# Attention weights times v in eighths of the TensorE array: blocks of 32 keys by 64 queries, four PSUM banks, keys in even and odd blocks, v by way of memory, and a new placing of all steps

## The chip, the cores and the metric

The kernel runs on one core of one Trainium2 chip. The metric is the device time of one execution in microseconds (us), and the time shown for a kernel is the median of its runs. The program is written by hand for the five engines of a core: PE (TensorE, matrix multiplies), DVE (VectorE), ACT (ScalarE), POOL (GpSimd) and SP (SyncE, which here issues all the transfers).

## The reference

The input is 2048 tokens of 128 channels. Twelve transformer layers (six, then a linear-attention block, then the same six again) work on it. One of the twelve layers, cut to what matters here:

```
def local_attention(q, k, v):            # 16 heads of 64; windows of 32 tokens
    bk2, bv2 = look(bk), look(bv)        # each window sees itself and the window before
    sim  = einsum('bhwie,bhwje->bhwij', bq, bk2) * 8.0     # 32 queries x 64 keys
    sim  = where(mask, -max, sim)        # key at most the query, and at most 32 back
    attn = softmax(sim, -1)
    out  = einsum('bhwij,bhwje->bhwie', attn, bv2)         # weights times v

def attn_layer(x, Wqkv, qs, ksc, Wo):
    q, k, v = split(x @ Wqkv)            # each 2048 x 1024
    q, k = l2norm(q) * qs, l2norm(k) * ksc, both rotated
    return local_attention(q, k, v) @ Wo

for i in range(6):
    x = attn_layer(shift_tokens(x), ...) + x
    x = ffn_layer(shift_tokens(x), ...) + x      # layer norm, gated GELU
```

The change is in the last line of `local_attention` and in what prepares its operands. Everything is float32, but for a band mask in bf16.

## The kernel before

Activations lie transposed, channels on the 128 partitions. A layer is worked in 8 chunks of 256 tokens (`AC`), a chunk in 4 steps: two halves of 128 tokens, `t`, times two groups of 8 heads, `h8`. Twelve layers of 32 steps make 384 steps. A feed-forward block of 512 tokens is spread over 8 steps (two chunks), so the work repeats every 8 steps.

For each step the kernel does, in the functions named: `project` (L288) multiplies one quarter of q and k out of the activations into two PSUM tiles, p0 for q and p1 for k; DVE multiplies each by the rotary table (`prod`, L297), POOL adds the halves (`abq`, `abk`, L303), ACT squares them (L309) and POOL adds the squares (L323), whose sums over channels `square_sums` takes on PE (`ss`, L331). `values_proj` (L347) computes half of v for 128 tokens, and ACT copies it (L351). `similarities` puts the mask (L475) and then q times k (L485) into two PSUM tiles, and DVE takes the maxima (L497, L498). `exponentials` (L510) is called for each of the two tiles: four ACT instructions each, called e0 and e1 below. `normalised` divides (`e`, L522, POOL), `transposed` turns the weights on PE (`te`, L535) and copies them (`eT`, L541). `values` (L562) multiplies weights by v into PSUM tiles `av`, which ACT and DVE copy to `oT` (L569, L571). In every second step `output` (L578) multiplies `oT` by Wo into `y`. The feed-forward's matmuls are `mean`, `var`, three gates and three ups `pf` (L612), and `yf` (L637).

In `values` the array is used as four tiles of 64 rows by 64 columns. One instruction takes 64 keys and 32 queries of one head; 32 of them make a step. The trace shows two passes for each, since float32 takes two. v has to lie on the partitions of the keys of each query window; `values_windows` makes these shifted copies by eight transfers from SBUF to SBUF for each 128 tokens.

Every PSUM tile but the similarities and the square sums comes from one pool of five banks:

```
ps_small = ctx.enter_context(tc.tile_pool(name="ps_small", bufs=5, space=PSUM))
def small(name):
    return ps_small.tile([P, CH], F32, tag="small", name=name)
```

A matmul that opens a tile waits until the last reader of the bank's earlier tile is done. The similarities have two banks, that is one pair, so the next step's mask waits for e0 and e1 of this one.

The order on each engine is written out by hand: the table `POS` gives each piece of each function a step, counted from its chunk's, and a place in that step; pieces are emitted in the order of these numbers, and every engine runs its instructions in that order. A generator's pieces go in turn whatever their own numbers say. In the kernel before, a step's places run: `ss` 25, `pv` 26, rotary products and squares of the projection before 42 to 48, `te` 62, `sim` 73, v's copy 90, e0 95, e1 96, `e` 108, `y` 112, `av` 149, the next projection 150, POOL's square sums 156, the copies of `av` 189 and 190.

Of the kernel before, what the change touches and what calls it, by code (L numbers as in the profile page):

```python
# [15 lines left out]
P = 128  # L16
# [17 lines left out]
    "tabq": [(-11, 129), (-10, 188)],  # L34
    "tabk": [(-9, 19), (-9, 166)],
    "ss": [(-6, 25)],
    "vwin": [(0, 76)],
    "gq0": [(-6, 100)],
    "gq1": [(-4, 78)],
    "e0": [(0, 95)],  # L40
    "e1": [(0, 96)],
    "nrm": [(1, 108)],
    "qn": [(-3, 127)],
    "ek": [(-1, 91)],
    "proj": [(-9, 150), (-8, 42), (-8, 44), (-8, 45), (-8, 48), (-8, 156)],
    "vproj": [(-2, 26), (-2, 90)],
    "norms": [(-4, 47), (-4, 82), (-4, 125)],
    "rk": [(-4, 206), (-3, 27)],
    "sk0": [(-2, 94)],
    "sk1": [(-1, 176)],  # L50
    "te": [(2, 62), (2, 64)],
    "av": [(2, 149), (2, 189), (2, 190)],
    "out": [(4, 112), (4, 134)],
    "sim": [(0, 73), (0, 74), (0, 75)],
    "ff": [(11, 101), (12, 34), (12, 106), (13, 7), (13, 170), (14, 131), (15, 124), (15, 143),
        (16, 17), (16, 42), (16, 143), (16, 159), (17, 51), (17, 140), (17, 192), (18, 50),
        (18, 58), (18, 148), (18, 162), (21, 146), (21, 199)],
    "ff2": [(12, 128), (12, 194), (13, 179), (14, 65), (14, 99), (15, 52), (15, 118), (15, 147),
        (16, 20), (16, 23), (16, 122), (16, 123), (16, 130), (16, 151), (16, 152), (16, 153),
        (16, 203), (17, 5), (17, 40), (17, 97), (17, 169)],  # L60
    "ff3": [(10, 182), (10, 184), (10, 186), (10, 194), (10, 198), (10, 200), (10, 204), (11, 2),
        (11, 4), (11, 13), (11, 24), (11, 35), (11, 36), (11, 37), (11, 120), (11, 133),
        (11, 139), (11, 157), (11, 181), (11, 183), (11, 193)],
    "start0": [(-19, 114), (-17, 104), (-16, 84), (-16, 168), (-13, 41), (-10, 79)],
    "start1": [(-11, 126), (-9, 70), (-7, 31), (-7, 142), (-7, 158), (-6, 141)],
    "start2": [(-9, 19), (-7, 29), (-5, 136), (-5, 205), (-4, 11), (-4, 121)],
    "start3": [(-4, 12), (-4, 16), (-4, 46), (-4, 88), (-3, 6), (-2, 28)],
    "sums0": [(-9, 1), (-9, 49), (-8, 43), (-8, 165), (-8, 174), (-7, 43), (-7, 137), (-6, 30)],
    "sums1": [(-1, 92), (-1, 119), (0, 72), (0, 77), (1, 38), (1, 39), (2, 161), (2, 184)],
    "sums2": [(1, 185), (1, 201), (2, 167), (2, 202), (3, 63), (3, 93), (3, 160), (4, 113)],  # L70
    "sums3": [(3, 195), (4, 15), (4, 80), (4, 81), (4, 144), (4, 145), (4, 177), (4, 191)],
    "kv": [(5, 3)],
    "outs0": [(5, 9), (5, 14), (5, 109), (5, 111), (5, 173), (5, 175), (6, 54), (6, 68), (6, 71),
        (6, 138), (7, 55), (7, 61), (7, 69), (7, 135)],
    "outs1": [(6, 60), (11, 83), (11, 110), (12, 18), (13, 53), (13, 67), (13, 180), (14, 98),
        (14, 163), (15, 32), (15, 56), (15, 102), (15, 154), (17, 87)],
    "outs2": [(6, 10), (13, 21), (13, 89), (13, 164), (14, 171), (14, 178), (14, 196), (15, 33),
        (15, 116), (15, 143), (16, 66), (16, 85), (16, 132), (17, 22)],
    "outs3": [(5, 172), (15, 115), (15, 155), (16, 117), (17, 86), (17, 105), (18, 8), (18, 103),
        (18, 107), (18, 162), (18, 197), (19, 57), (19, 59), (19, 187)],  # L80
# [14 lines left out]
def kernel(ctx: ExitStack, tc: tile.TileContext, a: dict, out: bass.AP):  # L95
# [65 lines left out]
    band = keep([P, 2, SK], "band", BF16, a["band"])  # L161
# [111 lines left out]
    def project(l, c, g):  # L273
# [8 lines left out]
        xs = xa[:, c * AC : (c + 1) * AC]  # L282
        both = []
        for s in range(2):
            ps = small(f"p{s}_{nm}")
            both.append(ps.rearrange("p (u t) -> p u t", u=2))
            for u in range(2):
                nc.tensor.matmul(  # L288
                    both[s][:, u, :], wqk[g][:, 2 * s + u, :], xs, start=True, stop=True
                )  # L290
# [46 lines left out]
    def values_proj(l, c, i):  # L337
# [5 lines left out]
        if j == 0:  # L343
            d["v", t] = work.tile([P, INNER], F32, tag="v", name=f"v_{nm}", bufs=3)
# [8 lines left out]
    def values_windows(l, c, t):  # L353


        d = chunk(l, c)
        ti = 2 * c + t
        nm = f"{d['nm']}_{t}"
        v = d["v", t]
        w = work.tile([P, 3, CH], F32, tag="vw", name=f"vw_{nm}", bufs=2)  # L360
        vp = None if ti == 0 else d["v", 0] if t else chunks[l, c - 1]["v", 1]
        for u in range(2):
            r, cols = 64 * u, slice(CH * u, CH * u + CH)
            if ti == 0:
                nc.gpsimd.memset(w[r : r + 32, 0, :], 0.0)
            else:
                nc.sync.dma_start(w[r : r + 32, 0, :], vp[96:P, cols])
            nc.sync.dma_start(w[r + 32 : r + 64, 0, :], v[0:32, cols])
            nc.sync.dma_start(w[r : r + 64, 1, :], v[32:96, cols])
            nc.sync.dma_start(w[r : r + 64, 2, :], v[64 - r : P - r, cols])  # L370
        d["vs", t] = [
            [w[0:64, 0], v[0:64, 0:CH], w[0:64, 1], w[0:64, 2]],
            [w[64:P, 0], w[64:P, 2], w[64:P, 1], v[64:P, CH:]],
        ]

    def gather(l, c, qk, g2):
# [3 lines left out]
        off = 0 if qk == "q" else WIN  # L380
        if g2 == 0:
            d["h" + qk] = work.tile(
                [P, 8, off + AC], F32, tag=f"h{qk}", name=f"h{qk}_{d['nm']}"
            )
        for j in range(2):
            src = d[qk, g2][64 * j : 64 * j + 64]
            first = 4 * g2 + 2 * j
            if qk == "q":
                nc.sync.dma_start(
                    d["hq"][:, first : first + 2, :].rearrange("p i t -> p (i t)"),  # L390
                    src.rearrange("p u i t -> p u (i t)"),
                )
            else:
                for i in range(2):
                    nc.sync.dma_start(d["hk"][:, first + i, WIN:], src[:, :, i, :])
# [54 lines left out]
    def earlier_keys(l, c):  # L450

        d = chunk(l, c)
        first = d["hk"][:, :, 0:WIN]
# [5 lines left out]
        nc.tensor.matmul(ps3, rot_m, chunks[l, c - 1]["hk"][:, :, AC:], start=True, stop=True)  # L459
        nc.scalar.copy(first, ps3)  # L460

    def similarities(l, c, step):
# [8 lines left out]
        masks = [(0, b) for b in range(4)] + [(1, 0)] * (2 * c + t == 0)  # L471
        for m, b in masks:
            for par in range(2):
# [4 lines left out]
                    start=(m == 0), stop=False, skip_group_check=True,  # L478
                )
        for i in range(4):  # L480
            for b in range(4):
                for par in range(2):
                    rows = slice(64 * par, 64 * par + 64)
                    at = t * P + WIN * b
                    nc.tensor.matmul(  # L485
                        sims[par][WIN * b : WIN * b + WIN, i, :],
                        d["hq"][rows, 4 * h8 + i, at : at + WIN],
                        d["hk"][rows, 4 * h8 + i, at : at + SK],
# [11 lines left out]
    def exponentials(l, c, step, par):  # L500
        d = chunk(l, c)
        t, h8 = divmod(step, 2)
        if par == 0:
            d["e", step] = work.tile(
                [P, 4, 2, SK], F32, tag="e", name=f"e_{d['nm']}_{step}", bufs=3
# [3 lines left out]
        for i in range(4):  # L509
            nc.scalar.activation(  # L510
                e[:, i, par, :], d["sims", step][par][:, i, :], AF.Exp,
# [5 lines left out]
    def normalised(l, c, step):  # L517
# [3 lines left out]
        ef = d["e", step].rearrange("p i r k -> p (i r) k")  # L521
# [435 lines left out]
```

## Time and profile before

| | |
|---|---|
| median of 3 runs (lowest, highest) | 3454.14 us (3449.54, 3456.67) |
| the profiled execution: its time, its span | 3449.61 us, 3447.8 us |
| mean granted TensorE clock | 0.982 of full speed |
| busy share of the span: PE, DVE, ACT, POOL | 96%, 77%, 72%, 63% |
| moved by DMA | 459.91 MB, 133 GB/s over the span |

The span is the time from the first to the last instruction; the execution is 1.8 us longer. A row of the groups of instructions gives engine, operation, output and inputs with their shapes, the count, the busy time, the mean time of one, and the idle time of the engine before them with what ended it. In a timeline, rows give start, length, engine, line, operation and count. PEld is the weight load of a matmul, which the trace keeps apart.

### The profile page before, as it was taken

To read this page: it belongs to the slowest core of one execution; us is meant where nothing else is said; L and a number is where in the kernel's file an instruction comes from. 1 tells how busy PE (TensorE), PEld (TensorE's weight loads), DVE (VectorE), ACT (ScalarE), POOL (GpSimd) and SP (SyncE) were. 2 spreads that over 40 slices of the span, in tenths; PEclk is the share of its full clock that TensorE was granted. 3 is DMA by queue.
4 is the path that set the end of the run, shared out by engine and by line. 5 is a ranking of instruction groups with operands and counts; after the bars stand their busy time and mean duration, and the time that the engine had idled before them with its cause. 6 is when DMAs were issued, how large, how long until landed. Compare 5 with 4: busy or idle time off the path is not lost. (4 is left out here: it accounts for less than half of the span.)

```text
span 3447.8 us, 153348 instructions
## 1 busy us (share of the span) xinstructions
PE 3293.9 (96%) x64088; PEld 2280.2 (66%) x64088; DVE 2658.6 (77%) x5068; ACT 2491.0 (72%) x8613; POOL 2182.2 (63%) x2195
## 2 busy tenths in 40 slices
PE   6999999999999999999678999999999999999998
PEld 3776776676667676676334766766767766766665
DVE  5787888878778788786446887887878888787785
ACT  4777777777777777776446777777777777777775
POOL 6766666667667667663136766666666666666661
PEclk8999999999999999999889999999999999999999
DMA  4665565556556556554004665566565565565552
GB/s 134 145 150 135 141 152 142 136 150 147 133 146 153 132 143 156 139 135 121 28 13 100 144 150 142 135 153 147 133 153 143 135 153 142 139 150 138 144 134 73
DMA packets 356445, 459.91 MB, mean 133 GB/s; under 512 B 52396, under 2 KB 218664, under 8 KB 355752
## 3 DMA queue, kind: packets, MB, share of 16 engines
q1 hardware_dynamic: 355752, 450.11, 53.7%
q8 instruction: 504, 8.26, 1.0%
q14 instruction: 189, 1.55, 0.1%
HBM read 96.53 MB, written 2.62 MB: 29 GB/s over the span
## 5 line engine op out<-in xcount | busy, mean ns | idle before, releaser
L510 ACT ACTIVATE e<-sim,st,rq 128x64 f32<-128x64 f32 x3072 | 1196.0, 410 | 352.6 <-DVE st L498 322.8
L297 DVE TENSOR_TENSOR prod<-p,tab 128x1024 f32<-128x1024 f32 x768 | 936.1, 1222 | 293.4 <-ACT sq L309 202.1
L288 PE MATMUL p<-xa,wqk 128*128 128x256 f32 x3072 | 776.5, 395 | 13.6 <-DVE xa L242 4.8
L303 POOL TENSOR_TENSOR abq<-prod 128x512 f32<-128x512 f32 x384 | 490.7, 1278 | 398.3 <-DVE prod L297 364.3
L522 POOL TENSOR_TENSOR e<-e,st 128x512 f32<-128x512 f32 x384 | 451.8, 1177 | 425.5 <-DVE st L520 242.8
L309 ACT ACTIVATE sq<-p 128x512 f32<-128x512 f32 x768 | 438.8, 603 | 350.5 <-PE ss L331 159.2
L303 POOL TENSOR_TENSOR abk<-prod 128x512 f32<-128x512 f32 x384 | 492.4, 1282 | 242.6 <-DVE prod L297 217.8
L510 ACT ACTIVATION_READ_ACCUMULATOR e<-sim,st,rq 128x1 f32 x3072 | 643.3, 209 | 0.0
L288 PEld LDWEIGHTS p<-xa,wqk 128*128 128x128 f32 x3072 | 557.7, 191 | 105.8 <-issue 9.8
L323 POOL TENSOR_TENSOR sq<-sq 128x256 f32<-128x256 f32 x768 | 580.1, 776 | 0.2
L562 PEld LDWEIGHTS av<-eT,vw 64*64 64x64 f32 x18432 | 392.3, 135 | 227.8 <-ACT hk L460 59.6
L562 PE MATMUL av<-eT,vw 64*64 64x32 f32 x18432 | 434.9, 221 | 2.9 <-DVE eT L541 1.8
L347 PE MATMUL pv<-wv,xa 128*128 128x512 f32 x768 | 417.5, 626 | 7.8 <-DVE oT L571 7.8
L578 PE MATMUL y<-oT,wo 128*128 128x128 f32 x3072 | 390.5, 280 | 0.2 <-DVE oT L571 0.2
L578 PEld LDWEIGHTS y<-oT,wo 128*128 128x128 f32 x3072 | 362.5, 192 | 36.1 <-issue 22.6
L562 PE MATMUL av<-eT,v 64*64 64x32 f32 x6144 | 384.3, 219 | 0.0
L535 PEld LDWEIGHTS te<-sq_consts,e 128*128 128x128 f32 x1536 | 188.5, 141 | 236.1 <-issue 166.9
L497 DVE TENSOR_REDUCE sim<-sim 128x4 f32<-128x256 f32 x768 | 325.9, 424 | 21.6 <-PE sim L485 20.7
L485 PE MATMUL sim<-hk,hq 64*32 64x64 f32 x24576 | 333.3, 223 | 0.1
L562 PEld LDWEIGHTS av<-eT,v 64*64 64x64 f32 x6144 | 318.8, 135 | 0.0
L612 PE MATMUL pf<-xc,w 128*128 128x512 f32 (+1 forms) x576 | 304.6, 615 | 11.5 <-POOL xc L600 9.3
L485 PEld LDWEIGHTS sim<-hk,hq 64*32 64x32 f32 x24576 | 306.0, 105 | 0.3
(140 smaller groups left out, 4270.9 us busy)
## 6 DMA issues: line engine op xcount, KB each, us to landing
hq<-abq SPq DMA_DIRECT2D x384, 256.0 KB
hk<-abk SPq DMA_DIRECT2D x768, 128.0 KB
vw<-v SPq DMA_DIRECT2D x768, 128.0 KB
rk<-rkd SPq DMA_DIRECT2D x384, 128.0 KB
vw<-v SPq DMA_DIRECT2D x744, 64.0 KB
wqk<-in_Wqk SPq DMA_DIRECT2D x48, 256.0 KB
tab<-in_rot SPq DMA_DIRECT2D x24, 512.0 KB
wv<-in_Wv SPq DMA_DIRECT2D x24, 256.0 KB
```

The costliest lines, as they stand in the source:

```text
L288: nc.tensor.matmul(both[s][:, u, :], wqk[g][:, 2 * s + u, :], xs, start=True, stop=True)
L297: nc.vector.tensor_tensor(prod, both[s].unsqueeze(2).to_broadcast([P, 2, 2, AC]), tabs[l, s].rearrange("p (u v) t -> p u v t", u=2), ALU.mult,
L303: nc.gpsimd.tensor_tensor(d["qk"[s], g // 2][:, :, g % 2, :], prod[:, 0], prod[:, 1], ALU.add)
L309: nc.scalar.activation(sq, both[s], AF.Square)
L323: nc.gpsimd.tensor_tensor(sq[:, 0, :], sq[:, 0, :], sq[:, 1, :], ALU.add)
L347: nc.tensor.matmul(ps, xa[:, ti * P : (ti + 1) * P], wv[j], start=True, stop=True)
L485: nc.tensor.matmul(sims[par][WIN * b : WIN * b + WIN, i, :], d["hq"][rows, 4 * h8 + i, at : at + WIN], d["hk"][rows, 4 * h8 + i, at : at + ...
L497: nc.vector.tensor_reduce(peaks[par], sims[par], AX.X, ALU.max, negate=True)
L510: nc.scalar.activation(e[:, i, par, :], d["sims", step][par][:, i, :], AF.Exp, bias=st8[:, 0, i, par : par + 1], scale=rq[:, i, par : par ...
L522: nc.gpsimd.tensor_tensor(ef, ef, st8[:, 1].rearrange("p i r -> p (i r)").unsqueeze(2).to_broadcast([P, 8, SK]), ALU.mult,)
L562: nc.tensor.matmul(av[u][r : r + 64, m, WIN * b : WIN * b + WIN], d["vs", t][u][b][:, at : at + DH], d["eT", step][64 * u : 64 * u + 64, i ...
L578: nc.tensor.matmul(y[:, 0:P], wo[:, i, :], d["oT", t].rearrange("p h u m q -> p (h u m) q")[:, i, :], start=(i == 0), stop=(i == 7),)
```

## The change

- `values`: the array is used as eight tiles of 32 rows by 64 columns. Row group j of four holds heads 4i+j; one instruction takes one block of 32 keys and those 64 queries that see it (32 at the two ends), and adds into the bank of its row group. There are 40 instructions in a step instead of 32. They write four PSUM tiles of 128 by 128 (av0 to av3) instead of two of 128 by 256, and four copies empty them: av0, av1 on ACT, av2, av3 on DVE.
- `values_windows`: v goes to a buffer in memory by one transfer of 512 KB and comes back by four of 128 KB, five transfers instead of eight, in two pieces.
- Keys lie by even and odd blocks of 32: `project` reads the activations in that order for k, the tables of k are permuted, the keys of the chunk before stand at the end of `hk`, and `similarities` takes its 64 keys as two runs of 32. The mask has three forms instead of two.
- `exponentials` writes each row as two runs of 32, and `normalised` and `transposed` take the new shape of `e`.
- The columns of Wv and the rows of Wo are ordered anew on the host.
- Buffers: v has 2 instead of 3, the copies of v 4 instead of 2 (4 KB a partition instead of 6 KB).
- `POS` is new throughout. A step's places now run: `te` 16, `sim` 21, `ss` 27, the maxima 59 and 65, `av` 61 (one step later than before), projection 68, norms 72, e0 74, the copies of `av` 76 (ACT) and 77 (DVE), `e` 78, rotary product of q 79, squares of k and of q 82 and 83, rotary product of k 85, e1 95, `y` 103, `pv` 143, POOL's square sums 156, v's copy 160.

```
 POS = {
-    "vwin": [(0, 76)],
+    "vwin": [(-1, 2), (0, 173)],
-    "e0": [(0, 95)],
-    "e1": [(0, 96)],
-    "nrm": [(1, 108)],
+    "e0": [(0, 74)],
+    "e1": [(0, 95)],
+    "nrm": [(1, 78)],
-    "proj": [(-9, 150), (-8, 42), (-8, 44), (-8, 45), (-8, 48), (-8, 156)],
-    "vproj": [(-2, 26), (-2, 90)],
-    "norms": [(-4, 47), (-4, 82), (-4, 125)],
+    "proj": [(-8, 68), (-8, 79), (-8, 83), (-8, 85), (-8, 82), (-8, 156)],
+    "vproj": [(-3, 143), (-3, 160)],
+    "norms": [(-4, 41), (-4, 72), (-4, 112)],
-    "te": [(2, 62), (2, 64)],
-    "av": [(2, 149), (2, 189), (2, 190)],
-    "out": [(4, 112), (4, 134)],
-    "sim": [(0, 73), (0, 74), (0, 75)],
+    "te": [(2, 16), (2, 26)],
+    "av": [(3, 61), (3, 76), (3, 77)],
+    "out": [(4, 103), (4, 146)],
+    "sim": [(0, 21), (0, 59), (0, 65)],
...
     def values_windows(l, c, t):
-        w = work.tile([P, 3, CH], F32, tag="vw", name=f"vw_{nm}", bufs=2)
-        vp = None if ti == 0 else d["v", 0] if t else chunks[l, c - 1]["v", 1]
-        for u in range(2):
...
-            nc.sync.dma_start(w[r + 32 : r + 64, 0, :], v[0:32, cols])
-            nc.sync.dma_start(w[r : r + 64, 1, :], v[32:96, cols])
-            nc.sync.dma_start(w[r : r + 64, 2, :], v[64 - r : P - r, cols])
+        out = dram.tile([4, WIN, 4, AC], F32, tag="vd", name=f"vd_{d['nm']}_{t}")
+        nc.sync.dma_start(out.rearrange("b p j f -> (b p) (j f)"), v)
+        yield
+        w = work.tile([P, 4, AC], F32, tag="vw", name=f"vw_{d['nm']}_{t}", bufs=4)
+        for j in range(4):
+            nc.sync.dma_start(
+                w[WIN * j : WIN * j + WIN], out[:, :, j, :].rearrange("b p f -> p b f")
+            )
+        d["vs", t] = w
...
     def values(l, c, step):
-        av = [
-            small(f"av{u}_{nm}")[:, 0 : 2 * P].rearrange("p (m q) -> p m q", q=P)
-            for u in range(2)
-        ]
-        for m in range(2):
-            for b in range(4):
-                for x in range(2):
-                    for u in range(2):
...
-                        nc.tensor.matmul(
-                            av[u][r : r + 64, m, WIN * b : WIN * b + WIN],
-                            d["vs", t][u][b][:, at : at + DH],
-                            d["eT", step][64 * u : 64 * u + 64, i, WIN * b : WIN * b + WIN],
-                            start=True, stop=True,
-                        )
-        yield
-        nc.scalar.copy(d["oT", t][:, h8, 0], av[0])
-        yield
-        nc.vector.tensor_copy(d["oT", t][:, h8, 1], av[1])
+        av = [small(f"av{j}_{nm}")[:, 0:P] for j in range(4)]
+        vs = d["vs", t]
+        before = vs if c + t == 0 else d["vs", 0] if t else chunks[l, c - 1]["vs", 1]
+        turns = ((vs, 0, 0, 64), (vs, 1, 32, 96), (vs, 2, 64, P), (before, 3, 0, 32), (vs, 3, 96, P))
+        for n, (v, b, lo, hi) in enumerate(turns):
+            for a2 in range(2):
+                for j in range(4):
+                    rows = slice(32 * j, 32 * j + 32)
+                    at = (2 * h8 + a2) * DH
+                    nc.tensor.matmul(
+                        av[j][64 * a2 : 64 * a2 + 64, lo:hi],
+                        v[rows, b, at : at + DH],
+                        d["eT", step][rows, 2 * (b % 2) + a2, lo:hi],
+                        start=(n == 0), stop=(n == 4), skip_group_check=True,
+                    )
+        for j in range(4):
+            if j % 2 == 0:
+                yield
+            (nc.vector.tensor_copy if j > 1 else nc.scalar.copy)(d["oT", t][:, h8, j], av[j])
```

## The prediction

> **What bounds the kernel now.** I read the page's busy shares first, then the steady stretch by windows, PE's timeline, the waits, and last the waits that the two built programs carry.
>
> ```profile
> PE 3293.9 (96%) x64088; PEld 2280.2 (66%) x64088; DVE 2658.6 (77%) x5068; ACT 2491.0 (72%) x8613; POOL 2182.2 (63%) x2195
> ...
> 1001.60:1067.40 65.80, 65.01 (x1327) 45.74 (x1326) 55.63 (x103) 48.57 (x172) 46.16 (x50) 1.00 0.61 154
> ...
> PEld te L535 <- ACT oT L569: 51.8, 42, 1.9
> PEld ss L331 <- POOL sq L323: 120.1, 206, 4.0
> ACT e L510 <- DVE st L498: 322.8, 245, 3.2
> ```
>
> PE bounds it. The window holds eight steps, 65.8 us, PE busy for 65.0 of them; 384 steps at that pace are 48 x 65.8 = 3158 of the 3448 us span, the rest being start, end and the linear block. Waits for `oT` and for the square sums exist but are small.
>
> ```profile
> 1004.38 1.02 PE L612 MATMUL pf<-xc,w 128*85 128x512 f32 x2
> 1005.34 0.32 PE L562 MATMUL av<-eT,vw 64*64 64x32 f32 x8
> ...
> 1006.40 1.99 PE L288 MATMUL p<-xa,wqk 128*128 128x256 f32 x8
> 1008.23 1.02 PE L347 MATMUL pv<-wv,xa 128*128 128x512 f32 x2
> 1009.09 0.60 PE L535 MATMUL te<-sq_consts,e 128*128 128x128 f32 x4
> 1009.62 0.30 PE L475 MATMUL sim<-band,ident_b 64*32 64x256 bf16 x8
> ```
>
> From start to start, in us: av 1.06, both projections 1.83 to 1.92, pv 0.86, te 0.53; likewise mask and similarities 0.89, y 1.88, one gate or up, mean or var 0.95, yf 2.75, nt 0.47, pk 0.54, ss 0.57. Eight steps of these sum to about 64.4, so PE waits only about 1.4 in 65.8.
>
> The chain that matters after the change is this, from a step in which nothing held it up:
>
> ```profile
> 1034.79 0.30 PE L475 MATMUL sim<-band,ident_b 64*32 64x256 bf16 x8
> ...
> 1036.29 0.16 DVE L498 TENSOR_TENSOR st<-sim,rq 128x4 f32<-128x4 f32 x1
> ...
> 1036.54 0.40 ACT L510 ACTIVATE e<-sim,st,rq 128x64 f32<-128x64 f32 x1 [1.30 <-DVE st L498]
> 1038.09 0.41 ACT L510 ACTIVATE e<-sim,st,rq 128x64 f32<-128x64 f32 x1
> 1039.62 0.39 ACT L569 COPY oT<-av 128x256 f32<-128x256 f32 x1
> ```
>
> e0 starts 1.75 after the step's mask (1036.54 - 1034.79), and each four exponentials take 1.54. It can hardly start earlier: similarities, maximum and product lie before it.
>
> **The change part by part.**
>
> *The av block.* Passes on one tile follow each other, those on different tiles overlap. Before: 32 instructions, 64 passes, 16 on each of four tiles, about 58 ns a pass (0.91 us from the first start to the last, 1005.34 to 1006.25, over some 15.7 passes), about 28 for 64 columns of weights and 30 for 32 queries; with 0.15 to drain, 1.06. After: 40 instructions, 80 passes, ten on each of eight tiles: six of 64 queries (28 + 56 = 84 ns) and four of 32 (58), 0.74, and with the drain about 0.87. So -0.19 a step, 384 x 0.19 = -73 us if nothing else moves. A rule speaks against it. The trace has matmuls on different tiles much closer than the Trainium skill allows ("TensorE: Matmul & The Clock Gate", "Wait — 56ns, not 53.3ns?"): starts never less than about 25 ns apart. The rows have 64 passes in 1.06 us, 16.6 ns each, and the similarities 64 in 0.77, 12 ns. By the rule 80 passes take 2.0 us, 1.1 more a step than I take; I follow the trace, and keep the rule for the upper end.
>
> *Copies.* A copy of 128 elements is, from 392 ns at 256 (oT) and 592 at 512 (v), an estimated 0.29 on ACT; on DVE (420 and 681) 0.29 too. Two each instead of one: +0.19 on ACT, +0.16 on DVE a step, 73 and 61 us, beside PE. Both engines stay under 80%; as throughput this costs nothing.
>
> *Order and banks.* This is what decides. A step takes four of five banks for av, and the next two openings are the projections. In the order before, the copies of av stood after e1 and p1 waited for v's copy, which precedes e0. Now ACT runs norms, e0, av's two copies, squares of k and q, e1, v. In the built program the first matmul on PE that needs an ACT copy of the same step's av0 is, over the eight steps: y, pf, p1, p1, y, p0, p1, and only in the last one late enough (pk). So PE, once per step, waits for e0 to end: 1.75 + 1.54 + 0.29 and some 0.1 of signals, 3.67 after the mask; PE itself has reached p1 by 0.89 + 0.87 + 0.96 = 2.72 (3.29 with ss). Queued behind the waiting matmul is the rest of the step on PE, and through p1 also ACT's squares, e1, DVE's product of k and POOL's sums. Phase by phase, counting from the feed-forward's second gate, from the start of the mask:
>
> - 0 (norms, ss, y): the norms' three ACT instructions (0.39 each) stand before e0 and wait for ss; e0 at 3.4, y needs the copies at 5.5, PE is there at 4.6. With 0.3 at ss: 1.3 lost.
> - 1 (Gelu): ACT has two table loads and three Gelus, 1059.78 to 1064.33 in the timeline, 4.55, between v's copy and e0; e0 at 4.8, `pf` waits until 6.7, PE is there at 4.15: 2.5.
> - 2 and 3: p1 until 3.7 or 4.05: 0.75 (0.7 of it at ss) and 0.95.
> - 4 (norms, ss, y): ss 1.2, y 1.0: 2.2.
> - 5: layer norm's Ln, Exp, Square (2 us) before e0, which starts at 2.15; p0 itself waits, until 4.0 instead of 1.76: 2.2.
> - 6: 0.8. 7: none.
>
> The losses at ss are POOL's: the square sums of a projection now come in the same step as its matmul, after `e`, `abq` and `abk` (1.2 + 1.3 + 1.3), and end some 8.7 after the mask; ss of the next step is there at about 8.4. Before, they had a step more.
>
> Sum: 10.7 us of new waits in eight steps, less 8 x 0.19 = 1.5, less the 1.4 that PE waits now: +7.8, times 48 = +374.
>
> *The clock.* PE has had no such gaps in steady state. Where it had, at the start:
>
> ```profile
> 41.20:44.60 3.40, 1.73 (x10) 0.57 (x9) 2.66 (x4) 1.94 (x5) 3.40 (x5) 0.99 0.64 154
> 44.60:48.00 3.40, 3.40 (x9) 2.35 (x8) 3.39 (x4) 3.27 (x7) 3.21 (x3) 0.50 0.00 0
> ```
>
> The column before DMA's is the granted clock: 1.67 us of idleness in a window of 3.4 and the next 3.4 ran at half. The Trainium skill (same page, "HAM oscillation — how this bites in real kernels") asks for a gap above about 3.4 us; by it no wait here counts, +0. By the row, gaps of 2.5 and 2.2 hit in about 7 of 10 phases of the window, and phase 4's pair in some 4 of 10: 1.8 windows in eight steps at 1.7 us lost, 3.0, or +146. I take 2.2, +106, as part falls where PE waits anyway.
>
> *v by way of memory.* SP issues 5 transfers instead of 8 per 128 tokens, 1024 KB instead of 768, so about +49 MB on 460. The write is issued right after v's copy, the read over a step later, the use two steps after that, some 20 us; the trace's other path through memory (`rk`) made SP wait at most 2.4 us. Cost 0, hidden by those two steps; if late it would hold all of PE, which the upper end covers. Fewer issues on SP put nothing later: k's and q's transfers are needed a step after they are issued.
>
> *At nothing:* the strided reads of xa, hk and e in runs of 32, 24 memsets fewer on POOL (12 us, not on the path), the third mask form, POOL's `e` in its new shape. The nearest row is the mask, which reads 4 runs of 64 at full pace. Bounds -12 to +40 (a tenth of p1); I take 0. Most sits before a wait that would hide it.
>
> Total on the span: 3448 + 374 + 106 = 3928, 3930 as an execution; the median of the runs shown stands 4.5 above the profiled one. I say 3930.
>
> **The rivals.**
> - *PE stays the bound, faster.* The place is the first opening after av, the price -73 us: 3380. It decides if ACT's copies are done before PE comes to p1, that is if e0 starts no later than about 0.8 after the mask. For it: PE is 96% busy, ACT 72%. Against: not one e0 in the steady stretch that I looked at starts before 1.7. 5%. In between, no change: 1%.
> - *Half of it.* Waits overlap or a phase catches up, clock at full: half of 10.7 remains, (5.3 - 2.9) x 48 = +115: about 3565, spread 3480 to 3700. For it: the phases are added from nominal starts. 14%.
> - *Worse.* Tiles at 25 ns a pass: what the waits don't hide is about 3.0 in eight steps, +145; or v's copies late: 4080 to 4250. For: the rule, and DMA already 0.61 busy. 10%.
> - *The tiles do not run eight at a time* (the change not doing what it says): 80 passes at 16.6 ns, 1.33: hidden in seven of eight steps, so within the main case.
>
> **How the numbers follow.** Main case 70%, 3930, its own range 3760 to 4080. The range 3660 to 4120 leaves out the faster and equal cases (6%), most of the half case (10%) and the upper end (5%). Faster by over 0.2%: 0.05, within 0.2% (7 us, about what a measurement can tell from no change): 0.01, slower: 0.94.
>
> **What would show it.** In the profile after: PE below 90% busy; waits PE (or its loads) <- ACT oT of some 300 us, on p, y and pf; ss <- POOL up; the av block 0.8 to 0.9 from start to start; granted clock under 0.97 with half windows in the steady stretch; ACT's e0 still 1.7 or more after the mask. It would be wrong if eight steps take under 66 us, if PE's waits end at DVE copies, or if the av block takes 1.1 or more.

## The result and the profile after

The changed kernel takes 3916.97 us, the median of four runs (3908.5 to 3929.93), against 3454.22 us of the kernel before on the same chip: a ratio of 1.1345, 95% interval 1.1311 to 1.1378. The forecast was 3930, with a range of 3660 to 4120. The total came out; several of its terms did not, and they are taken apart below.

The page of the kernel after, busy time of each engine with its share of the span, and the larger of two DMA queues that the profile labels "instruction" (packets, MB, share of the DMA engines):

```profile
PE 3374.2 (86%) x70232; PEld 2354.3 (60%) x70232; DVE 2709.5 (69%) x5452; ACT 2507.3 (64%) x8997; POOL 2267.1 (58%) x2171
...
q8 instruction: 553, 9.06, 1.0%
```

PE is at 86% where it had 96%, and no other engine is near its limit. Eight steps by windows (window; its length, then busy time of PE, weight loads, DVE, ACT, POOL; granted clock; DMA share; GB/s):

```profile
1002.45:1078.01 75.56, 66.85 (x1459) 47.87 (x1458) 54.50 (x111) 50.41 (x185) 44.33 (x40) 0.98 0.51 135
```

Where eight steps took 65.80 with PE idle for 0.79, they take 75.56 with PE idle for 8.71. What PE waited for, by the waits (us in total, times, longest):

```profile
PE ss L335 <- POOL sq L327: 122.6, 110, 5.5
PE p L294 <- ACT oT L567: 112.9, 151, 2.0
PE pf L608 <- ACT oT L567: 96.9, 44, 2.4
PE av L558 <- issue: 53.7, 48, 2.7
...
PE y L574 <- ACT oT L567: 6.7, 7, 1.5
```

and the same waits before, as far as there were any:

```profile
PE ss L331 <- POOL sq L323: 25.7, 15, 3.5
PE te L535 <- ACT oT L569: 20.0, 33, 1.1
...
PE av L562 <- issue: 1.0, 2, 0.8
```

Three things are in the list of the kernel after: `ss` for POOL's square sums, p and pf for ACT's copy of av, and a third that the prediction does not have, gaps inside the av block for which the profile shows no wait at all ("issue"). Phase 1 (counted as in the prediction) has the longest wait for a copy; the timelines of PE and ACT:

```profile
1068.13 0.30 PE L470 MATMUL sim<-band,ident_b 64*32 64x256 bf16 x8
...
1074.48 0.43 ACT L567 COPY oT<-av 128x128 f32<-128x128 f32 x2
...
1074.80 1.13 PE L608 MATMUL pf<-xc,w 128*128 128x512 f32 x2 [2.42 <-ACT oT L567]
```

`pf` opens 6.67 us after the step's mask, as ACT's copies end. Phase 5 has such a wait, a gap in av, and what follows from them:

```profile
1029.29 0.30 PE L470 MATMUL sim<-band,ident_b 64*32 64x256 bf16 x8
1029.41 0.84 PE L483 MATMUL sim<-hk,hq 64*32 64x64 f32 x64
1030.18 0.96 PE L558 MATMUL av<-eT,vw 32*64 32x64 f32 x69
1032.09 0.33 PE L558 MATMUL av<-eT,vw 32*64 32x32 f32 x11 [0.94 <-issue]
1033.31 3.56 PE L294 MATMUL p<-xa,wqk 128*128 128x256 f32 x8 [0.89 <-ACT oT L567]
```

PE stops for 0.94 us after 69 of the 80 matmuls of av, with nothing named; then it waits 0.89 for ACT's copy; then the two projections take 3.56 us instead of 1.99. The windows show the clock in that time (the column before the DMA share is the granted clock):

```profile
1029.68:1033.09 3.41, 1.79 (x136) 1.53 (x119) 2.08 (x8) 3.34 (x12) 0.94 (x2) 1.00 0.59 189
1033.09:1036.50 3.41, 3.19 (x8) 2.57 (x9) 1.05 (x2) 0.33 (x3) 1.05 (x1) 0.50 0.54 133
```

A window of 3.41 us with PE idle for 1.62 is followed by one at half clock. The sum over the whole execution, from the trace: PE stands still for 530 us where it did for 145 (+385); the time at half clock goes from 128 to 327 us, and reckoned as half of PE's busy time in it, PE lost 133 us where it had lost 48 (+85); the work itself, reckoned at full clock, is 3241 us where it was 3246 (-5). That makes +465 of the +466 between the spans (3914.2 and 3447.8).

### The profile page after: what moved, and what is told of

It reads as the page before. It is cut to its first block, busy times and chain, and to the rows that moved or that the text cites. A ratio compares the mean times of both kernels' runs of the same rounds, so it can differ in the third digit from the quotient of the medians.

```text
span 3914.2 us, 165986 instructions
## 1 busy us (share of the span) xinstructions
PE 3374.2 (86%) x70232; PEld 2354.3 (60%) x70232; DVE 2709.5 (69%) x5452; ACT 2507.3 (64%) x8997; POOL 2267.1 (58%) x2171
## 5 line engine op out<-in xcount | busy, mean ns | idle before, releaser
L294 PE MATMUL p<-xa,wqk 128*128 128x256 f32 x3072 | 836.9, 411 | 135.5 <-ACT oT L567 112.9
L523 POOL TENSOR_TENSOR e<-e,st 128x512 f32<-128x512 f32 x384 | 405.3, 1055 | 835.8 <-DVE st L520 763.8
L307 POOL TENSOR_TENSOR abq<-prod 128x512 f32<-128x512 f32 x384 | 570.1, 1485 | 318.0 <-DVE prod L301 310.7
L307 POOL TENSOR_TENSOR abk<-prod 128x512 f32<-128x512 f32 x384 | 550.5, 1434 | 286.4 <-DVE prod L301 242.3
L509 ACT ACTIVATION_READ_ACCUMULATOR e<-sim,st,rq 128x1 f32 x3072 | 672.3, 219 | 0.0
L558 PE MATMUL av<-eT,vw 32*64 32x64 f32 (+1 forms) x30720 | 459.9, 228 | 67.1 <-issue 53.7
L558 PEld LDWEIGHTS av<-eT,vw 32*64 32x64 f32 x30720 | 407.9, 130 | 170.6 <-issue 96.7
L608 PE MATMUL pf<-xc,w 128*128 128x512 f32 (+1 forms) x576 | 331.3, 663 | 106.9 <-ACT oT L567 96.9
L537 DVE COPY eT<-te 128x512 f32<-128x512 f32 x384 | 264.0, 688 | 101.4 <-PE te L533 98.1
L355 ACT COPY v<-pv 128x512 f32<-128x512 f32 x384 | 230.8, 601 | 155.2 <-PE pv L351 155.0
```

Source lines behind the costliest of these rows:

```text
L294: nc.tensor.matmul(to, wqk[g][:, 2 * s + u, :], xs[s], start=True, stop=True)
L307: nc.gpsimd.tensor_tensor(d["qk"[s], g // 2][:, :, g % 2, :], prod[:, 0], prod[:, 1], ALU.add)
L509: nc.scalar.activation(e[:, :, 2 * i + par, :], d["sims", step][par][:, i, :].rearrange("p (n k) -> p n k", k=WIN), AF.Exp, bias=st8[:, 0, ...
L523: nc.gpsimd.tensor_tensor(e, e, sums.to_broadcast([P, 2, 8, WIN]), ALU.mult)
L558: nc.tensor.matmul(av[j][64 * a2 : 64 * a2 + 64, lo:hi], v[rows, b, at : at + DH], d["eT", step][rows, 2 * (b % 2) + a2, lo:hi], start=(n ...
L608: nc.tensor.matmul(ps, w1[:, s, j * P : j * P + size[j]], x, start=True, stop=True)
```

## The experiments

Twelve kernels. All times are medians of four runs, but for the last row, which is one run; ratios are to the kernel before, which stood at 3449 to 3454 us in every group of runs. The table gathers PE's waits from each profile, in us; "in av" is the gap inside the av block with no wait shown; the last column is the time that the trace has at half clock.

| kernel | time | ss for POOL | any op for oT | in av | time at half clock |
|---|---|---|---|---|---|
| before | 3454 | 26 | 31 | 1 | 128 |
| after | 3917 | 123 | 220 | 54 | 327 |
| all av copies on DVE | 3786 | 142 | 21 | 83 | 241 |
| ACT's copies before e0 | 3789 | 142 | 54 | 72 | 252 |
| av twice, one step in four | 4110 | 123 | 122 | 193 | 481 |
| new arithmetic, old places | 3862 | 24 | 133 | 36 | 413 |
| old arithmetic, new places | 3721 | 151 | 70 | 10 | 168 |
| gap filled, few instructions | 3980 | 119 | 134 | 47 | 246 |
| DVE copies, projection early | 4309 | 10 | 28 | 5 | 734 |
| DVE copies, ss late | 3726 | 6 | 20 | 144 | 317 |
| the same, te between | 3740 | 8 | 14 | 88 | 266 |
| old arithmetic, new places, ss late | 3653 | 9 | 63 | 69 | 229 |
| DVE copies, ss late, pv between | 3894 | 7 | 14 | 35 | 331 |
| half the queries in 48 of 80 passes (one run) | 3857 | 121 | 149 | 66 | 369 |

### All copies of av on DVE

```
-            (nc.vector.tensor_copy if j > 1 else nc.scalar.copy)(d["oT", t][:, h8, j], av[j])
+            nc.vector.tensor_copy(d["oT", t][:, h8, j], av[j])
```

> All four copies of av go on DVE, whose queue does not hold them behind e0; ACT's copies are gone. Theory (PE waits because two of the four banks are given back only behind e0 in ACT's queue): the waits on p, pf, y fall from about 10 us to 1 to 2 in eight steps, only the waits of ss for POOL stay, and the clock recovers with them: 3480 to 3600 us, and PE's waits for ACT's oT are gone from the list. Rival (POOL's late square sums or the sheer number of banks are what costs; ACT's place in it is incidental): over 3800, since POOL's order and the banks are as they were. Second rival (DVE becomes the new bound, 0.58 us a step more on it than with two copies moved off): the waits come back on DVE's oT, 3650 to 3800.

Measured: 3786.05 us, ratio 1.097 (1.0953 to 1.0986). That is 131 us faster than the kernel after, and outside what the theory and the first rival gave. It lies in the range of the second rival, but not by its mechanism: the waits for DVE's `oT` are 21 us. The waits of this kernel:

```profile
PE ss L335 <- POOL sq L327: 141.8, 148, 5.5
PE av L558 <- issue: 83.1, 71, 3.6
PE pf L608 <- ACT sq L313: 48.1, 42, 1.4
PE p L294 <- DVE oT L567: 19.1, 45, 1.2
```

ACT's copies are gone from the list, and 21 of the 220 us for `oT` are left; so the wait named in the prediction is real and hangs on ACT's queue. But PE's idle time fell only from 530 to 431 us: `ss`, the gaps in av, and `pf` for a bank that ACT's squares hold took about half of the 200 us that were freed. The step that was taken as deciding is one of several.

### ACT's copies in front of the norms and e0

```
-    "av": [(3, 61), (3, 76), (3, 77)],
+    "av": [(3, 61), (3, 70), (3, 77)],
```

> ACT's two copies of av are placed in front of the norms and of e0 instead of behind e0, nothing else. Theory (place in ACT's queue): av ends some 1.9 us after the mask, so the copies are done by about 2.6, before PE comes to p1 at 2.9; e0 moves to about 2.6 after the mask in the steps where it started at 1.75. 3500 to 3650 us. If the banks cost by their number and not by the order on ACT, or if e0 being late costs as much as it saves: 3800 or more.

Measured: 3788.53 us, ratio 1.0973 (1.0946 to 1.1), between the two readings. The same gain by the other road, and the same remainder (`ss` 142, gaps in av 72). ACT now waits itself, 826 us in all, for av to end, and e0 starts about 2.5 us after the mask in phases 3, 5 and 7 instead of 1.7 to 2.2. That e0 is later costs nothing that the total shows. Both runs together: place and engine of the copies are worth 130 us of 463, where the working had some 400 us of waits on them.

### New arithmetic in the old places

The table of places is put back whole; only the write of v, which the kernel before does not have, gets a place a step ahead of the reads. As elsewhere, `-` is the kernel after.

```
-    "vwin": [(-1, 2), (0, 173)],
+    "vwin": [(-1, 92), (0, 76)],
...
-    "av": [(3, 61), (3, 76), (3, 77)],
+    "av": [(2, 149), (2, 189), (2, 190)],
...
-    "sim": [(0, 21), (0, 59), (0, 65)],
+    "sim": [(0, 73), (0, 74), (0, 75)],
...
```

> The new arithmetic of av, its four banks and v by way of memory, but in the places of the kernel before (the write of v a step earlier than its reads). Theory (four banks cost only where ACT's copies stand behind e0 and PE needs the bank next): here the copies stand behind both e0 and e1 of the step, but av too comes late in it; PE then waits at te and pv for them, about 0.5 to 1 us a step: 3550 to 3750 us. If the placing alone made the loss: 3400 to 3480. If four banks cost what they cost wherever av stands: 3850 or more.

Measured: 3861.91 us, ratio 1.1187 (1.117 to 1.1204), as the last reading had it (3850 or more). `ss` is back at 24 us, as it was before, so those waits belong to the places. The four banks cost here too. In the waits of PE:

```profile
PE av L557 <- ACT v L354: 91.4, 43, 2.2
PE p L293 <- DVE oT L566: 79.7, 129, 2.7
PE p L293 <- ACT oT L566: 45.9, 135, 1.8
```

and in the timeline once in eight steps:

```profile
1034.44 1.10 PE L607 MATMUL pf<-xc,w 128*128 128x512 f32 x2
1035.47 0.55 PE L557 MATMUL av<-eT,vw 32*64 32x64 f32 x6
1038.19 1.46 PE L557 MATMUL av<-eT,vw 32*64 32x64 f32 x74 [2.16 <-ACT v L354]
```

av issues six matmuls and then stands for 2.16 us: it opens four banks, and one of them still holds a v that ACT, which runs the Gelus first, has not copied. That a block of four banks waits when it opens was not in my working, which had only what follows av waiting.

### Old arithmetic in the new places

The kernel before, with the table of the kernel after but for two lines:

```
-    "vwin": [(-1, 2), (0, 173)],
+    "vwin": [(0, 173)],
...
-    "vproj": [(-3, 143), (-3, 160)],
+    "vproj": [(-2, 143), (-2, 160)],
```

> The arithmetic of the kernel before (two banks for av, 32 instructions on 64x64 tiles, v's windows without memory) in the places of the kernel after; only v's projection comes a step later, as its windows need. Theory A (four banks are what costs; the places alone do not): p no longer opens on a bank that ACT still holds, PE's waits for oT all but go, the sums of POOL that now come late stay: 3560 to 3700 us. Theory B (the places alone cost most, the four banks little): 3750 or more. Theory C (the places are harmless): 3440 to 3500. A second reading: inside the av block, which has 64 instructions fewer for PE to fetch, the gaps with no wait shown (67 us in the kernel after) should fall below 25 us if the fetching of instructions makes them, and stay above 50 if not.

Measured: 3720.92 us, ratio 1.077 (1.0746 to 1.0795), just outside theory A's range, and no theory is right as it stood. The second reading came out: the gaps inside av fell from 54 to 10 us. It does not show its cause, though: with the wait at `ss` out of the way, the same arithmetic has 69 us of these gaps (below). The places alone cost 270 us; all the rest of the change, in the old places, 409; both together 463. So the two losses overlap, and cannot be added. Of the places the main wait is the one for POOL's sums:

```profile
PE ss L332 <- POOL sq L324: 151.3, 148, 6.4
PE pv L348 <- ACT oT L570: 56.7, 42, 1.5
...
PE av L563 <- issue: 9.6, 14, 1.9
```

### DVE copies, and the projection early

The places of the first and of the linear block go back to those of the kernel before too, since the projection reads what they write.

```
-    "proj": [(-8, 68), (-8, 79), (-8, 83), (-8, 85), (-8, 82), (-8, 156)],
+    "proj": [(-9, 150), (-8, 42), (-8, 44), (-8, 45), (-8, 48), (-8, 156)],
```

> All copies of av on DVE, as in the earlier run (3786 us), and besides it the q and k projections in the places of the kernel before, over half a step earlier, with the places of the first and of the linear block that go with them. Theory (what is left after the copies moved are POOL's square sums, which come in the same step as the projection: 138 us at ss, and the half clock behind it): ss no longer waits, p opens late enough after av that no bank is missed: 3500 to 3640 us. Rival (POOL's sums are not what the loss hangs on, waits move to te or av instead): 3720 to 3830.

Measured: 4309.32 us, ratio 1.2471 (1.2406 to 1.2536), far outside both ranges. The waits at `ss` did go, from 142 to 10 us. Instead:

```profile
PE av L557 <- ACT sq L312: 521.4, 347, 2.4
```

```profile
1005.95 0.34 PE L557 MATMUL av<-eT,vw 32*64 32x64 f32 x6
1007.80 1.04 PE L557 MATMUL av<-eT,vw 32*64 32x64 f32 x74 [1.51 <-ACT sq L312]
```

With the projection ahead of av, its two banks are still being squared on ACT when av wants four of five. It happens in nine steps of ten (347 of 384). The banks are the scarce thing here: with av soon behind a projection it waits itself, and with av right before one, the order of the change, the projection waits for its copies.

### The gaps in av: what fills them, and what does not

Three runs bear on the gaps with no wait shown. The first was made for the clock. In every fourth step the av block is computed twice:

```
-        for n, (v, b, lo, hi) in enumerate(turns):
+        for n, (v, b, lo, hi) in [*enumerate(turns)] * (2 if step == 2 else 1):
```

> In every fourth step (the two of eight with the longest waits) the av block is computed twice into the same banks; the output is the same, PE has 96 blocks of about 1 us more to do, and they lie right before its long waits. Theory of the clock (idleness of over half of a 3.4 us window puts the next window at half): the two longest gaps, 2.2 to 2.5 us, shrink to about 1.3, half of the 326 us at half clock go, and the kernel gets 40 to 120 us faster although it does more, 3800 to 3880. Rival (the half clock falls where PE waits anyway, or the gap has to be longer to count): the same within 20 us, as the added blocks hide in the waits. Second rival (the copies that release the banks start later with the second block): 3930 to 4015.

Measured: 4109.66 us, ratio 1.1904 (1.1886 to 1.1922), slower than any theory gave: 96 blocks of 1.02 us are 98 us of work, and the kernel lost 193. The wait of pf for `oT` all but went (96.9 to 3.5 us), as was meant, but

```profile
PE av L558 <- issue: 192.6, 108, 3.6
```

the gaps inside av went from 54 to 193 us. By phases it is the doubled blocks that have them: in phases 1 and 5 together they went from 27 to 158 us. The second run fills the same idle time with three large matmuls, six records instead of 80:

```
-        av = [small(f"av{j}_{nm}")[:, 0:P] for j in range(4)]
+        banks = [small(f"av{j}_{nm}") for j in range(4)]
+        if step == 2:
+            for _ in range(3):
+                nc.tensor.matmul(banks[0][:, 0 : 3 * P], ident,
+                                 sq_consts.rearrange("p a b -> p (a b)"), start=True, stop=True)
+        av = [b[:, 0:P] for b in banks]
```

> The kernel after, with three matmuls of 128x384 (some 1.9 us in six instructions) written into the first bank of av ahead of the av block in every fourth step, the two of eight with the longest waits; av then overwrites them and the output is the same. It fills idle time with work and few instructions, where doubling the av block filled it with many. Theory of the clock (idleness inside a 3.4 us window brings the next one to half): the time at half clock falls from 327 us to 150 to 230 and the kernel gets 40 to 100 us faster, 3815 to 3880, with 180 us more of PE's work. Rival (half clock does not come from these gaps): time at half clock within 40 us of 327, the kernel the same or slower, 3910 to 4000. Second reading: with 1.9 us between the similarities and av, the gap inside the av block in those steps, with no wait shown, goes (67 us falls below 25) if it is PE running out of fetched instructions.

Measured: 3979.63 us, ratio 1.153 (1.1508 to 1.1553), 63 slower than the kernel after, with 177 us more of PE busy. The time is in the rival's range; the time at half clock fell by 81 us to 246, more than the rival allowed and less than the theory gave. In the filled steps both went as the theories had it: in phases 1 and 5 together, half clock fell from 160 to 27 us and the gaps in av from 27 to 1. In the other steps both rose, half clock from 116 to 174 us, for which no run gives the cause, and the gaps from 27 to 46. Phase 5:

```profile
1040.43 2.20 PE L551 MATMUL av<-sq_consts 128*128 128x384 f32 x6
1042.57 1.09 PE L563 MATMUL av<-eT,vw 32*64 32x64 f32 x80
1043.96 1.99 PE L294 MATMUL p<-xa,wqk 128*128 128x256 f32 x8 [0.30 <-ACT oT L572]
```

av runs through, the wait is 0.30, and p takes 1.99 where it took 3.56. The net failed in part because phase 1 did not give its idle time back: some 101 us of work went in (48 times 2.1), and the waits for `oT` there fell only from 97 to 64 us. In 42 of 48 such steps it is now p that waits for ACT's copy, where it was pf, so the banks are dealt out differently. So this run shows the half clock following the idle time, and does not give a clean price for it.

The third cuts each pass of 64 queries to 32, and so leaves out of the sums the earlier block of keys in three windows of four:

```
-        turns = ((vs, 0, 0, 64), (vs, 1, 32, 96), (vs, 2, 64, P), (before, 3, 0, 32), (vs, 3, 96, P))
+        turns = ((vs, 0, 0, 32), (vs, 1, 32, 64), (vs, 2, 64, 96), (before, 3, 0, 32), (vs, 3, 96, P))
```

> The kernel after, with each of the 64-query passes of av cut to 32 queries, so that the earlier block of each window's two is left out of the sums; same number of instructions, tiles and banks. If each tile's own weights and streaming set the pace of the block (28 + 30 ns a pass, ten to a tile), it goes from 1.02 to about 0.75 us from start to start. If a pass can't start less than some 12 ns after the one before, whatever it streams (as the similarities' 64 in 0.77 us), it stays at 0.96 to 1.05. The kernel's time should hardly move either way, within 40 us of 3917, since the block is followed by waits.

Measured, in one run: 3856.8 us, 60 less than the kernel after and outside the 40 allowed. Its waits of p for `oT` are lower (47 instead of 113): p1 in phase 3 opens 3.12 us after the mask instead of 3.60, p0 in phase 5 at 2.54 instead of 4.01, so the banks must be dealt out differently there, and the time says little. The block itself:

```profile
1003.92 1.04 PE L558 MATMUL av<-eT,vw 32*64 32x32 f32 x80
1004.89 2.06 PE L294 MATMUL p<-xa,wqk 128*128 128x256 f32 x8
```

0.97 us from start to start, against 1.02 with twice the queries in 48 of the 80 passes (the medians over the execution, in the phases without gaps, are the same). So what a pass streams hardly sets the pace: 80 passes at 12.1 to 12.8 ns each, as the similarities' 64 at 12. What does set it, no run shows; every pass has a weight load of its own.

### DVE copies, ss behind the projection

```
-    "ss": [(-6, 27)],
-    "norms": [(-4, 41), (-4, 72), (-4, 112)],
+    "ss": [(-6, 70)],
+    "norms": [(-4, 80), (-4, 94), (-4, 112)],
```

> All copies of av on DVE, as in the first of these runs (3786 us), and besides it the matmuls of ss behind the projection instead of in front of av, with the norms that read them after e0 instead of before it. Theory (what is left after the copies moved is mostly POOL's late square sums, which hold PE at ss for 138 us and hold e0 behind the norms in two steps of eight, and the half clock that follows): ss no longer holds PE before av, e0 of those two steps starts about 2 us after the mask instead of 4.6 and 5.4: 3560 to 3660 us. Rival (the steps' length is set by a loop of ACT, DVE and POOL and PE only shows it): ss waits as long in its new place or the wait goes to te or p, 3740 to 3830.

Measured: 3725.64 us, ratio 1.0805 (1.0784 to 1.0826), 60 us better than with the copies alone. Between the two expectations. `ss` waits for 6 instead of 142 us, and e0 of the two steps with norms starts 2.9 and 2.4 us after the mask instead of 4.6 and 5.4. The wait did not go to te or p. It went to

```profile
PE av L558 <- issue: 144.2, 111, 2.9
```

```profile
1013.68 0.35 PE L470 MATMUL sim<-band,ident_b 64*32 64x256 bf16 x8
1013.80 0.88 PE L483 MATMUL sim<-hk,hq 64*32 64x64 f32 x64
1014.61 0.70 PE L558 MATMUL av<-eT,vw 32*64 32x64 f32 x39
1017.07 0.69 PE L558 MATMUL av<-eT,vw 32*64 32x64 f32 x41 [1.76 <-issue]
```

mask, similarities and av now follow each other without a stop, 152 matmuls and as many weight loads, and PE stands for 1.76 us in the middle. The trace has the transfers of the instruction queue q8, 16 KB each. They come at PE's pace: one for 254 of its matmuls and weight loads, in the kernel before (504 transfers) as in the kernel after (553). One started at 1014.67 and landed at 1015.63, and PE went on 1.44 us later. It is so for nearly all gaps above 0.3 us inside av that have no named wait: 93 of 96 end 1.1 to 1.7 us after such a transfer has landed. Of the 45 with a named wait 3 do, and of moments taken at random over the span 9 in 100 lie so.

### The same with te, and with pv, between the similarities and av

```
-    "te": [(2, 16), (2, 26)],
+    "te": [(2, 58), (2, 64)],
```

> The same with te's four transposes between the similarities and av. Theory (PE runs out of fetched instructions where mask, similarities and av, 304 instructions with their weight loads, come in some 2.2 us): the gaps inside the av block without any wait fall from some 90 us to below 40, and the kernel is 20 to 60 us faster than the one with ss late alone. Rival (0.53 us between does nothing for the fetching, or te then waits for POOL's e): within 20 us of that kernel, or slower.

Measured: 3740.33 us, ratio 1.0835 (1.0817 to 1.0853): the rival, within 20 us. The gaps in av fell from 144 to 88, not below 40, and the mask's wait for e0 and e1 rose from 18 to 52. The other run leaves te where it was and moves pv:

```
-    "vproj": [(-3, 143), (-3, 160)],
+    "vproj": [(-3, 58), (-3, 62)],
```

> Copies on DVE and ss late (3726 us), and besides it v's projection (pv, 0.86 us in a handful of instructions) between the similarities and av, its copy on ACT before e0. Theory (PE runs out of fetched instructions in the run of mask, similarities and av; time with few instructions ahead of av lets a fetch land): the gaps inside av without any wait, 171 us, fall below 90, and with them part of the half clock: 3600 to 3690 us. Rival (the gaps hang on something else, or move to the next dense block as they did with te between): the gaps, in av and the mask together, stay above 140, 3700 to 3780.

Measured: 3893.86 us, ratio 1.1285 (1.1264 to 1.1305), 168 us slower than without it and outside both ranges. The gaps agree with the theory; the time does not:

```profile
PE sim L470 <- ACT e L509: 105.2, 160, 3.6
PE p L294 <- ACT v L355: 88.5, 42, 2.1
PE av L558 <- issue: 34.9, 40, 1.9
```

The gaps with no wait shown fell from 144 to 35 us (all gaps above 0.3 us in av from 171 to 69) once about 1 us with few instructions stood between the dense blocks. But v's copy now stands before e0 on ACT, which puts e0 later by 0.8 us in the quiet steps, so the mask waits for the similarities' banks, and p for v's bank.

### Old arithmetic, new places, ss late

The edit of ss and norms above, on the kernel with the old arithmetic in the new places.

> The old arithmetic with two banks in the new places (3721 us), with ss and the norms moved in the same way. If the places cost only by POOL's late square sums (145 us at ss, and what hangs on them), 3480 to 3580; if something else in the places costs too, 3640 to 3740. Against the kernel with four banks, copies on DVE and ss late it shows once more what the new arithmetic costs with that wait out of the way.

Measured: 3652.64 us, ratio 1.0589 (1.0553 to 1.0625), 68 us faster than without it and on the second reading: something else in the places costs too. Of its waits, 69.3 us are again gaps in av with no wait shown (9.6 while `ss` still held PE in front of av), and all 40 of those above 0.3 us end 1.1 to 1.7 us after an instruction transfer; 55 us are `pv` waiting for ACT's `oT`, which no run removed. What else the places cost is not taken apart. Against the kernel with the new arithmetic, copies on DVE and ss late (3726), the new arithmetic costs 73 us with the waits at `ss` out of the way; the two differ in where the copies are made as well.

No kernel of these beats the kernel before; the nearest is 6% slower.

## Why the prediction was right, point by point

- *What bounds the kernel after: right.* PE at 86%, waiting, and nothing else busy above 69%. Of PE's +385 us of idleness, +189 are for `oT` (220 against 31), +97 at `ss`, +53 in the av block.
- *Step "The av block", -73 us: wrong.* The block went from 1.06 to 1.02 and not to 0.87, so -15. The failing term is "ten on each of eight tiles" at 84 and 58 ns: it takes the tiles as limited by their own weights and queries, and no row shows how the 58 ns divide into 28 and 30. By that term the run with half the queries should have had about 0.75; it has 0.97. The row to use stood in the working already, the similarities' 12 ns a pass: 80 x 12 = 0.96, and 0.06 more measured. By the Trainium skill's 25 ns between starts ("TensorE: Matmul & The Clock Gate", "Wait — 56ns, not 53.3ns?") the block would be 2.0. That section speaks of back-to-back matmuls and does not mention tiles side by side; the measurement decides.
- *Copies: right.* 282 ns on ACT and 283 on DVE, against 0.29, and beside PE.
- *Order and banks: the openings right, the waits too large.* With the copies off ACT, or ahead of e0, its waits go (220 to 21 and 54 us) and the kernel gains 130 us. The openings came where the working put them (medians, after the mask): `pf` in phase 1 at 6.68 us (6.7 forecast), p1 in phases 2 and 3 at 3.97 and 3.60 (4.05 and 3.67), p0 in phase 5 at 4.01 (4.0). But the sum had waits of about 400 us, that is 10.7 us in eight steps less 2.2 for `ss`, times 48, and 220 were measured (the signs that it gives say some 300). The term that was mis-sized is PE's own arrival: PE came later than reckoned, by the av block (1.02 to 1.26 for 0.87), by gaps in it and by `ss`, and the list of waits counts from the end of the matmul before, about 0.15 later than the start-to-start sums do. So `pf` in phase 1 waits 2.01 us on average (2.5 forecast), p0 in phase 5 1.40 (2.2), p1 in phases 3 and 6 0.25 and 0.32 (0.95 and 0.8), and `y` in phases 0 and 4 hardly at all (1.0 each).
- *The losses at ss: right in sum.* 2.2 us in eight steps times 48 is 106; `ss` waits 97 us more. Of its parts phase 4 came out (1.20 us on average, 1.2 forecast); phase 0 waits 0.71 for 0.3 and phase 2 0.04 for 0.7, which make up for each other by luck. e0 behind the norms was put at 3.4 and is at 4.6 in phase 0, and at 5.4 in phase 4, where no number was given.
- *Missing: the gaps with no wait shown, some 53 us more than before.* Nothing in the working reckoned what it takes to bring PE its instructions. The change both adds 16 passes and their weight loads a step to av and puts av right behind the similarities.
- *The clock: right in kind, +85 against +106.* A rule of a gap over some 3.4 us (same page, "HAM oscillation — how this bites in real kernels") would have given nothing for these waits, none of which in steady state is that long; the measurement decides. In the kernel after, of 48 windows at full clock with PE busy less than 45%, 47 were followed by half clock; of 41 between 45 and 55%, 20; of 940 above 60%, none. The +106 had been lowered from +146 by judgement.
- *v by way of memory, reads in runs, masks, at 0: nothing speaks against it.* In the list of waits av never waits for a transfer.
- *The total.* The prediction had -73 for the block and +447 of new waits less the old, +374 in sum; measured +380 (385 of idleness, -5 of work). The 1.4 us taken off as old waits came from sums of starts; the window row has PE idle for 0.79, which would have made the sum some 29 us larger. The gain was overrated by 58 to 68 us and the waits by about as much, so the total was nearer than its terms deserve: that it came within 13 us is luck. And one sentence fell: that the order of ACT's queue "is what decides". It decides 130 us. With it mended, PE meets `ss`, and with that mended, the instruction supply.

## What to carry to other kernels

A block that takes four of five PSUM banks made every neighbour wait here: what follows it, for its copies, and the block itself, for whoever held the banks before. Count who holds each bank at the time that the block opens, on both sides, before counting what the block saves. When several waits stand behind each other, removing the longest gives less than its length (131 of 200 us here, and 60 of 136 for the next), so forecast the second wait before promising the first. When the forecast of an opening is good and the wait is still wrong, look at when the waiting engine arrives. And a finer tiling that adds instructions is paid at the pace at which PE takes them, about 12 ns for each pass here, not at what a tile streams.

## What the runs showed of the hardware

- PE can run out of instructions; this is inferred, and no run changed the supply alone. Where mask, similarities and av stand together, 304 matmuls and loads in some 2 us, PE stood for 1.1 to 1.3 us on average, and up to 2.9, with no wait shown. One 16 KB instruction transfer comes for 254 matmuls and loads. Of the gaps above 0.3 us inside av with no named wait, 44 of 44 in the kernel after, 93 of 96 with ss late and 40 of 40 in the old arithmetic with ss late ended 1.1 to 1.7 us after one had landed. Work with few instructions ahead of the block made the gaps go (27 to 1 us in the filled steps, 144 to 35 with pv between), a doubled block made them larger (27 to 158 us), and the old arithmetic has fewer (69 against 144 with ss late). In the old places it is not so: 16 of 64 gaps end like that, and the rest stay unexplained.
- The pace of many small float32 matmuls on eight tiles of 32x64 or 64x32 was 12 to 13 ns a pass, whether a pass took 32 or 64 queries; on four tiles of 64x64 it was 16.6 (64 passes in 1.06 us).
- In the kernel after, the clock went to half after 47 of 48 windows of 3.41 us in which PE was busy for less than 45%, after 20 of 41 between 45 and 55%, and after none of 940 above 60%; idle time in two pieces below 1 us each was enough (1.79 of 3.41 us busy). It is not quite a rule: with the projection early, 23 of 821 windows above 60% were followed by half clock.
